# A planned list-and-sort graph kernel: smaller sort pieces with a pause behind each at the end, and a larger hop in the planner

## The chip, the cores and the metric

The kernel runs on one core of one Trainium2 chip. The metric is the device time of one launch in microseconds (us). The engines are called as in the profile: PE is TensorE, DVE is VectorE, ACT is ScalarE, POOL is GpSimd and SP is SyncE. Line numbers (L1332) are lines of the kernel before; the changed file has the same number of lines, so that they hold for both.

## The reference

The input is 16 graphs of 1024 nodes with 64 features each (`x`), a dense 0/1 adjacency matrix for each graph, a node mask (all ones here) and the weights of a small MLP. What is computed, cut to what matters:

```python
h = relu(layernorm(x))
neigh = (adj > 0) & ~eye
rank = exclusive cumsum of neigh along a row;  nb = neighbours of the row
skip = ceil(nb / 2) if nb > 10 else 1
rem = neigh & (skip > 1) & (rank % skip == skip - 1) & mask;  rem |= rem.T
nd = (adj with ones on the diagonal) without rem          # who is left, own node included
s = sort over the nodes left in nd of h, feature by feature
agg = 0.25 * q(s, 0.25) + 0.5 * q(s, 0.5) + 0.25 * q(s, 0.75)   # interpolated quantiles
out = h + agg
y = (relu(out @ W1 + b1) @ W2 + b2) * mask
return x + y
```

So each node gathers the feature rows of the neighbours that are left (some 9 of 1024), sorts them feature by feature, and takes a weighted sum of a few places of the sorted list.

## The kernel before

**Layout.** A batch is one graph. For each of the 16 batches `prepare` (a generator) turns the adjacency matrix into lists of neighbours: `load` (signs L961 on ACT, transposes L968 on PE), `drop` (the removed entries, L1038 to L1049), `keep` (L1061 to L1079), `order` (the nodes ordered by degree, L1085 to L1120) and `collect` (the lists of row numbers `idx`, L1141 to L1210, DVE's MAX8 work). `normalize` (L1255 to L1290) writes relu(layernorm(x)) to a table in DRAM, `gtab`.

**Gathers.** POOL then issues indirect DMAs (L1332 in `fetch`): each takes one column of a list `idx` and brings 128 rows of the table into one slot of a tile. The tiles of a pair of batches (there are 8 pairs) are `g0`, `g1`, `g4` and `g6`, by class of degree; `g0` and `g1` have two buffers, `g4` and `g6` one. The program has 986 gathers and scatters on POOL, and they run one behind the other nearly all the time. A 'place' below counts them from 0.

**Sorts.** `sort` (L1417) takes a tile through a fixed network of steps: minimum and maximum of slots, L1437, L1440 and L1445, on DVE in float32. Then the slots that count are multiplied by coefficients (L1462 on DVE, or L1460 on ACT for the last three pairs, `by_act`), and PE sums them up (L1466). A step over several slots is cut into pieces: most elements per partition in one instruction are `PART` = 384, or `WHOLE` = 1024 with `whole`. Without `whole`, each DVE instruction goes through `opened` (L855): it puts a memset of one column of a small tile `pause` (L859) right behind the instruction; nobody reads `pause`. With `whole` there is no such write. In the kernel before `whole` holds in two places: in `aggregate` (L1547) for the last pair of batches, and in `aggregate_group` (L1707) for the last of two groups. A group is the tile `gg`: the few nodes of a group of 8 batches that have more neighbours than the slots of `g0`.

**The end of the program.** The last pair is sorted in three parts: the tiles g0 and g1 with both batches, then g4 and g6 batch by batch, with the MLP of the first batch (`between` inside `results`) beside the second. Its first slots are not gathered but picked by one-hot matmuls on PE (`pick`, L1376 to L1413, whose DVE part is `hot`, L1392). Memsets (L1525, L1531) and ACT copies (L1528) fill slots ahead of each sort. Behind the last sort come ACT's weights (L1460), PE's sums, the sums by one-hot matrix (`at_p`, L1567 to L1572), two MLP matmuls with their copies, and the output DMA.

**What sets the order.** The program is written as interleaved generators, but the order of each engine's instructions is then set by a planner, `arrange` (L713): it takes all instructions, finds who must be before whom, and walks six times (`ROUNDS`) through the program with a modelled duration for each instruction (`Step.cost`, L605). `forward` (L674) starts at each moment the most urgent instruction that is ready, and `backward` (L695) does this from the end and thereby sets how urgent each is. The order of the best of the six forward walks is kept and tied to each engine. In both walks the time from the end of an instruction to the start of one that depends on it is `between` (L669):

```python
def between(s, o):
    return s.lag + 60 if o.engine != s.engine or s.moves else 115 if s.engine == "DVE" else 0
```

The `lag` is 200 ns for PE, 150 for ACT, 80 for DVE, 950 for a gather and 1500 and more for SP's transfers. So 60 ns stand for a hop between engines or behind a DMA. A pause is no instruction of its own for the planner: it is a tail that makes its instruction 12 ns longer. A 'leash' (`LEASH`) makes a gather wait for a DVE or ACT instruction that was planned to end 25 us before it.

Of the kernel before, what the change touches and what calls it, by code (L numbers as in the profile page):

```python
# [70 lines left out]
GROUP = 8  # L71
SLICE = P // GROUP
SECOND = 14
ROUNDS, LEASH = 6, 25000


TURNED = (0, 1, 3, 2, 0, 1, 3, 2)
# [475 lines left out]
ACTP, ACTB = 5, 13  # L553
# [114 lines left out]

def between(s, o):  # L669

    return s.lag + 60 if o.engine != s.engine or s.moves else 115 if s.engine == "DVE" else 0


def forward(steps, ranks):  # L674
# [138 lines left out]
def list_layer(  # L813
# [15 lines left out]
    B = x.shape[0]  # L829
# [489 lines left out]
    def fetch(m, classes=CLASSES, halves=(0, 1)):  # L1319

        for tiles, slots in classes:
            lo, n = tiles[0], len(tiles)
            held, order = PLANS[slots][:2]

            def begin(h, tiles=tiles, lo=lo, n=n, slots=slots, held=held):
                opening((tiles, slots), m)
                nc.scalar.copy(gathered[m, tiles][:, slots - 1, :, h], owns[m][:, lo:lo + n, h])

            issued, given_out = paced

            def gather(h, slot, k, at, tiles=tiles, lo=lo):
                ins = nc.gpsimd.indirect_dma_start(  # L1332
                    out=gathered[m, tiles][:, slot, k - lo, h], out_offset=None, in_=tables[2 * m + h][0],
                    in_offset=bass.IndirectOffsetOnAxis(ap=lists[2 * m + h][:, at:at + 1], axis=0),
                    element_offset=tables[2 * m + h][1], engine_sem=issued,
                )
                given_out[ins.ins.name] = ins
                return ins

            for h in halves:  # L1340
                queue.append(partial(begin, h))
                for k in tiles:
                    for s, slot in enumerate(order[:FULL[k] + ((k, FULL[k]) in HOSTS)]):
                        if m < pairs - 1 or s >= LEAST[k]:
                            queue.append(partial(gather, h, slot, k, PASSED[k] + s))
# [129 lines left out]
    def terms(acc, out):  # L1475

        for n in range(3):
            to = out[n]
            nc.scalar.copy(to, acc)  # L1479
            if n < 2:  # L1480
                nc.tensor.matmul(acc, minus16, to, start=False, stop=True, skip_group_check=True)
# [14 lines left out]
    def aggregate(m, o, between=None):  # L1496


        last = m == pairs - 1
        coef = coefs[m]  # L1500
        for half in (0, 1) if last else (1, 0):
            parts = CLASSES[2 * half:2 * half + 2][::1 if last else -1]
            for sides in ((0, 1), (1, 2)) if last and half else ((0, 2),):
                hs, one = slice(*sides), sides[0] if last and half else None
                if not one:
                    shape = [P, 4, 2, C] if one is None else [P, 2, 4, C]
                    tag, bufs = ("mx", 3) if last and not half else ("agg", 2)
                    whole = psum.tile(shape, F32, name="acc", tag=tag, bufs=bufs)
                    for tiles, slots in parts:
                        rows, own = slice(tiles[0] - 4 * half, tiles[-1] + 1 - 4 * half), gathered[m, tiles][:, slots - 1]  # L1510
                        nc.tensor.matmul(
                            whole[:, rows] if one is None else whole[:, :, rows], ident32,
                            own if one is None else own.rearrange("p n h c -> p h n c"),
                            start=((tiles, slots) == parts[0]), stop=False, skip_group_check=True,
                        )
                acc = whole if one is None else whole[:, one]
                if one is not None:
                    yield from between(one, False)
                line = {}
                for tiles, slots in parts:  # L1520
                    for k in tiles:
                        for s, slot in enumerate(PLANS[slots][1]):
                            line[k, s] = gathered[m, tiles][:, slot, k - tiles[0], hs]
                            if s >= FULL[k] and (k, s) not in HOSTS:
                                nc.vector.memset(line[k, s], BIG)  # L1525
                for host, guest, first, stop in GUESTS:
                    if host in line:
                        nc.scalar.copy(line[guest][first:stop], line[host][first:stop])  # L1528
                for host, lo, hi in BARE:
                    if host in line:  # L1530
                        nc.vector.memset(line[host][lo:hi], BIG)  # L1531
                for tiles, slots in parts:
                    lo, n = tiles[0], len(tiles)
                    g = gathered[m, tiles]
                    plan = PLANS[slots]
                    if one is None:
                        lines, weigh = g.rearrange("p s n h c -> p s (n h c)"), partial(
                            lambda s, many, lo, n: coef[:, s:s + many, lo:lo + n].rearrange("p s n h -> p s (n h)"),
                            lo=lo, n=n,
                        )  # L1540
                    else:
                        lines, weigh = g[:, :, :, one], partial(
                            lambda s, many, lo, n, h: coef[:, s:s + many, lo:lo + n, h], lo=lo, n=n, h=one
                        )
                    yield from sort(
                        lines, plan, window(tiles, slots)[0], weigh, acc[:, lo - 4 * half:lo - 4 * half + n],
                        m >= ACTP, last,  # L1547
                    )
                    if sides[1] == 2:
                        gathered.pop((m, tiles))  # L1550
                if half and not last:
                    for h in ((0, 1),) if m < pairs - 2 else ((0,), (1,)):
                        fetch(m + 1, CLASSES[2:], halves=h)
                terms(acc, [
                    o[:, 4 * half:4 * half + 4, hs if one is None else one, C * n:C * n + C] for n in range(3)
                ])
                if last and not half:
                    bring_back(m, o)
                if one is not None:
                    yield from between(one, True)  # L1560
# [133 lines left out]
    def aggregate_group(grp):  # L1694
        n = GROUP // 4
        gg = groups.pop(grp)
        to, xg = gathered.pop(("group", grp))
        coef = wk.tile([P, TOP, n], F32, name="gcoef", bufs=1)
        weights(coef, group_num[grp][:, :, 1], n, TOP)
        yield 1.0  # L1700
        tag, bufs = ("mx", 3) if grp == B // GROUP - 1 else ("agg", 2)
        acc = psum.tile([P, n, C], F32, name="gacc", tag=tag, bufs=bufs)
        nc.tensor.matmul(acc, ident32, gg[:, CAP - 1], start=True, stop=False, skip_group_check=True)
        for k in range(n)[::-1]:
            yield from sort(
                gg[:, :, k], PLANS[(CAP, SECOND + 1)[k]], window((0,), CAP)[0],
                lambda s, many: coef[:, s:s + many, k:k + 1], acc[:, k], whole=grp == B // GROUP - 1,  # L1707
            )
        o = wk.tile([P, n * C], F32, name="go", tag="lows", bufs=1)
        nc.scalar.copy(o, acc.rearrange("p k c -> p (k c)"))  # L1710
        yield 0.0
        tp = psum.tile([P, P], F32, name="ot", tag="misc")
        nc.tensor.transpose(tp, o, ident32)
        ot = wk.tile([P, P], F32, name="got", tag="h1", bufs=1)
        nc.scalar.copy(ot, tp)
        yield 0.0
        h1 = wk.tile([P, n, P], F32, name="gh1", tag="highs", bufs=1)
        for k in range(n):
            hp = psum.tile([P, P], F32, name="hp", tag="misc")
            nc.tensor.matmul(hp, w1[k * C:(k + 1) * C], ot[k * C:(k + 1) * C], start=True, stop=True)  # L1720
            nc.scalar.activation(h1[:, k], hp, AF.Relu, bias=b1c)
            yield 0.0
        output(h1.rearrange("p k r -> p (k r)"), n, group_num.pop(grp)[:, :, 0], xg)
        gathered["out", grp], gathered["sum", grp] = (to, xg), o
# [143 lines left out]
def window(tiles, n):  # L1868

    return min(LEAST[k] for k in tiles) // 4, -(-3 * (n - 1) // 4) + 1  # L1870
# [176 lines left out]
```

## Time and profile before

| what | value |
|---|---|
| median of 3 runs | 1443.4 us (1442.67 to 1445.76) |
| time of the profiled execution | 1448.98 us |
| its span in the trace | 1447.2 us |
| mean granted PE clock | 0.898 |
| DVE busy | 1220.1 us (84%) |
| PE busy | 1100.0 us (76%) |
| POOL busy | 1049.3 us (73%) |
| ACT busy | 1041.4 us (72%) |
| first gather on POOL starts, last one ends | 62.77 us, 1412.5 us |

The span runs from the first to the last instruction of the profiled execution. The profiled execution's own time is 1.8 us more than its span, and 5.6 us more than the median. The trace lists each instruction with start and duration; 'idle before' is the time that an engine stood still in front of an instruction, with the name of what ended it. A slice is one fortieth of the span, 36.2 us. Overlapping starts are normal on DVE: an instruction's record begins while the one ahead of it drains, so that the cost of one is read from start to start.

### The profile page before, as it was taken

How to read it: one execution, taken by the hardware profiler on the slowest of the kernel's cores; microseconds unless marked ns; L12 is line 12 of the kernel's file. 1: busy time of each engine (PE TensorE's matmuls, PEld its weight loads, DVE VectorE, ACT ScalarE, POOL GpSimd, SP SyncE). 2: the span in 40 equal slices, each digit the busy share in tenths (PEclk: the TensorE clock that was granted, in tenths of full speed). 3: DMA queues.
4: the chain of work that ended last, by engine and by line, in shares of the span. 5: the costliest groups of instructions: out<-in, count | busy, mean ns of one | idle time of the engine just before them, and what ended most of it. 6: DMA issues, size and time to landing. Idle time of an engine off the chain costs nothing. (4 is left out here: it accounts for less than half of the span.)

```text
span 1447.2 us, 30238 instructions
## 1 busy us (share of the span) xinstructions
PE 1100.0 (76%) x9011; PEld 706.0 (49%) x9011; DVE 1220.1 (84%) x5869; ACT 1041.4 (72%) x2869; POOL 1049.3 (73%) x991
## 2 busy tenths in 40 slices
PE   6877887999888985898479986599837995358167
PEld 4545555555555553555246554365514674125044
DVE  5646799978899899978799898998799779979765
ACT  8797698888959893879558773758839763449554
POOL 0277777777777777777777777777777777778880
PEclk9999998999999997899789997699969998669568
DMA  6453334333524252325332342422211111112110
GB/s 218 141 174 106 111 119 127 90 90 102 148 56 131 64 154 54 100 59 148 91 87 65 88 127 60 118 61 64 69 24 40 32 27 24 24 31 61 35 20 21
DMA packets 128831, 121.67 MB, mean 84 GB/s; under 512 B 95730, under 2 KB 96274, under 8 KB 128658
## 3 DMA queue, kind: packets, MB, share of 16 engines
q1 hardware_dynamic: 97106, 87.29, 19.9%
q0 software_dynamic: 31552, 32.36, 10.2%
q8 instruction: 73, 1.20, 0.3%
q14 instruction: 100, 0.82, 0.2%
HBM read 108.79 MB, written 9.05 MB: 81 GB/s over the span
## 5 line engine op out<-in xcount | busy, mean ns | idle before, releaser
L1332 POOL DMA_INDIRECT g<-gtab,idx x952 | 1013.1, 1064 | 354.3 <-DMA g<-gtab,idx 154.8
L1440 DVE TENSOR_TENSOR g<-g 128x384 f32<-128x384 f32 (+2 forms) x659 | 312.0, 494 | 25.3 <-DMA g<-gtab,idx 19.1
L1445 DVE TENSOR_TENSOR g<-g 128x384 f32<-128x384 f32 (+2 forms) x659 | 310.8, 493 | 5.5 <-DMA gg<-g 4.2
L1145 PE MATMUL codeP<-pack,perm 128*128 128x332 bf16 x1024 | 181.0, 318 | 54.3 <-DVE perm L1120 34.0
L1466 PE MATMUL acc<-g,kf 128*128 128x128 f32 (+2 forms) x472 | 137.6, 424 | 69.0 <-ACT g L1460 46.3
L1048 ACT ACTIVATE dist<-rk,bias 128x512 f16<-128x512 f32 x256 | 169.7, 723 | 23.8 <-DVE bias L1023 10.1
L1145 PEld LDWEIGHTS <-perm 128*128 128x128 bf16 x1024 | 94.1, 100 | 132.8 <-DVE perm L1120 48.2
L981 ACT ACTIVATE ne<-tp 128x512 fp8e4<-128x512 f32 x248 | 144.7, 640 | 12.5 <-PE tp L974 11.1
L1071 ACT ACTIVATE kept<-kp 128x512 fp8e4<-128x512 f32 x224 | 138.4, 642 | 14.3 <-PE kp L1066 5.8
L1460 ACT ACTIVATE g<-g,coef 128x64 f32<-128x64 f32 x336 | 89.2, 359 | 81.4 <-DVE g L1440 63.2
L968 PE MATMUL tp<-kb,sg 128*128 128x128 bf16 x1024 | 107.7, 232 | 47.9 <-ACT dist L1048 27.5
L961 ACT ACTIVATE sg<-at 128x1024 bf16<-128x1024 f32 x122 | 133.8, 1097 | 4.0 <-DMA at<-in_adj_dram 3.9
L1466 PEld LDWEIGHTS acc<-g,kf 128*128 128x128 f32 x472 | 81.5, 210 | 99.2 <-ACT g L1460 56.0
L1038 PE MATMUL rk<-kb,cnt 128*128 128x512 bf16 x256 | 102.2, 399 | 35.9 <-ACT dist L1048 24.1
L1043 PEld LDWEIGHTS <-ne 128*128 128x128 fp8e4 x1024 | 82.2, 101 | 86.0 <-issue 55.9
L859 DVE MEMSET pause<- 128x1 bf16 x2043 | 120.5, 59 | 0.0
L968 PEld LDWEIGHTS <-sg 128*128 128x128 bf16 x1024 | 79.9, 104 | 79.7 <-issue 57.5
L1043 PE MATMUL rk<-kw,ne 128*128 128x128 fp8e5 x1024 | 108.6, 227 | 0.0
L1158 ACT CAST st<-codeP 128x4 bf16<-128x4 f32 x128 | 21.4, 167 | 119.8 <-DVE rest L1156 88.2
L1066 PE MATMUL kp<-kw,rem 128*128 128x128 fp8e5 x1024 | 101.1, 219 | 0.0
L1061 PE MATMUL kp<-ne,kw 128*128 128x512 fp8e4 x256 | 97.5, 382 | 3.5 <-ACT dist L1048 1.4
L1062 PE MATMUL kp<-rem,kw 128*128 128x512 bf16 x256 | 97.5, 381 | 0.0
(202 smaller groups left out, 2371.6 us busy)
## 6 DMA issues: line engine op xcount, KB each, us to landing
at<-in_adj_dram SPq DMA_DIRECT2D x122, 512.0 KB
g<-gtab,idx POOLq DMA_INDIRECT x952
xt<-in_x_dram SPq DMA_DIRECT2D x16, 256.0 KB
y<-in_x_dram SPq DMA_DIRECT2D x16, 256.0 KB
gtab<-xt SPq DMA_DIRECT2D x16, 256.0 KB
out_dram<-y SPq DMA_DIRECT2D x14, 256.0 KB
spare<-in_adj_dram SPq DMA_DIRECT2D x6, 512.0 KB
gg<-g SPq DMA_DIRECT2D x32, 48.0 KB
```

The source lines that it names most:

```text
L859: tails[nc.vector.memset(pause[:, at:at + 1], 0.0).ins.name] = ins.ins.name
L961: nc.scalar.activation(sg, at, AF.Sign)
L968: run.append(nc.tensor.matmul(tp[:, s], sg[:, m * P:(m + 1) * P], ident16, start=(s == 0), stop=(s == 3 and t // 4 != n), skip_group_check ...
L981: nc.scalar.activation(to, tp, AF.Relu, saturate=False)
L1043: run.append(nc.tensor.matmul(rk[:, s * P:(s + 1) * P], ne[:, 4 * n + s, ts], upper, start=False, stop=(s == 3), skip_group_check=True,))
L1048: nc.scalar.activation(dist[:, n * HALF:(n + 1) * HALF], rk, AF.Abs, bias=bias[:, t:t + 1])
L1071: nc.scalar.activation(kept[:, 4 * n:4 * n + 4], kp, AF.Relu, saturate=False)
L1145: run.append(nc.tensor.matmul(flat, perm[:, t, k * P:(k + 1) * P], pack[:, t], start=False, stop=(t == NT - 1), skip_group_check=True,))
L1332: ins = nc.gpsimd.indirect_dma_start(out=gathered[m, tiles][:, slot, k - lo, h], out_offset=None, in_=tables[2 * m + h][0], in_offset=bass ...
L1440: nc.vector.tensor_tensor(at(f + k * df, df, many), pa, pb, OP.min if what == "<" else OP.max)
L1445: nc.vector.tensor_tensor(pa if back else pb, pa, pb, OP.max if what == "<" else OP.min)
L1466: nc.tensor.matmul(acc, ident32, lines[:, s], start=False, stop=(s == now[-1] and not ends), skip_group_check=True)
```

## The change

Three edits. In the planner the 60 ns of a hop become `LATE` = 300 ns, which changes the plan and so may change the order of every engine. The sorts of the last pair and of the last group are no longer `whole`: their pieces hold at most 384 elements per partition, and each of their DVE instructions gets its memset of `pause`.

```diff
-ROUNDS, LEASH = 6, 25000
+ROUNDS, LEASH, LATE = 6, 25000, 300
...
 def between(s, o):
 
-    return s.lag + 60 if o.engine != s.engine or s.moves else 115 if s.engine == "DVE" else 0
+    return s.lag + LATE if o.engine != s.engine or s.moves else 115 if s.engine == "DVE" else 0
...
                     yield from sort(
                         lines, plan, window(tiles, slots)[0], weigh, acc[:, lo - 4 * half:lo - 4 * half + n],
-                        m >= ACTP, last,
+                        m >= ACTP, False,
                     )
...
             yield from sort(
                 gg[:, :, k], PLANS[(CAP, SECOND + 1)[k]], window((0,), CAP)[0],
-                lambda s, many: coef[:, s:s + many, k:k + 1], acc[:, k], whole=grp == B // GROUP - 1,
+                lambda s, many: coef[:, s:s + many, k:k + 1], acc[:, k], whole=False,
             )
```

The two programs, compared instruction by instruction: DVE has 376 instructions more, 344 of them pauses (2387 instead of 2043) and 32 of them because 32 instructions of 128x768 on the last pair's `g1` become 64 of 128x384. The other engines have the same instructions, in another order.

## The prediction

> **What bounds the kernel now.** I read the page first, in part 1 and in the row of POOL in part 2 (tenths of a slice busy, 40 slices).
>
> ```profile
> span 1447.2 us, 30238 instructions
> ...
> PE 1100.0 (76%) x9011; PEld 706.0 (49%) x9011; DVE 1220.1 (84%) x5869; ACT 1041.4 (72%) x2869; POOL 1049.3 (73%) x991
> ...
> POOL 0277777777777777777777777777777777778880
> ...
> L859 DVE MEMSET pause<- 128x1 bf16 x2043 | 120.5, 59 | 0.0
> ```
>
> No engine is full on average, but POOL's row is flat at 7 from the second slice on. In the timeline of POOL the gathers start at 62.77 us and end at 1412.5 us, nearly always 0.30 us after one another; the longest other pause is 1.13 us. An undisturbed gather takes 0.94 us, 1.25 us from start to start. The 64 places from 920 (1301.64 us) to 984 (1412.53 us) take 110.9 us, 1.73 us each; the 920 before them (62.8 to 1301.6 us) took 1.347 us each, and in blocks of 40 between 1.27 and 1.46. So POOL's stream is the bound up to 1412 us, and at its end, where the unpaused sorts run, it is slower. The timeline of POOL there (start, duration, engine, line, in brackets the idle time in front):
>
> ```profile
> 1316.27 0.94 POOL L1332 DMA_INDIRECT g<-gtab,idx  x1 [0.30 <-ACT g L1413]
> 1317.51 3.48 POOL L1332 DMA_INDIRECT g<-gtab,idx  x1 [0.30 <-DVE y L1663]
> 1321.30 1.65 POOL L1332 DMA_INDIRECT g<-gtab,idx  x1 [0.31 <-DMA g<-gtab,idx]
> 1323.25 4.88 POOL L1332 DMA_INDIRECT g<-gtab,idx  x1 [0.30 <-DMA g<-gtab,idx]
> 1328.44 2.24 POOL L1332 DMA_INDIRECT g<-gtab,idx  x1 [0.30 <-DMA g<-gtab,idx]
> 1330.98 1.16 POOL L1332 DMA_INDIRECT g<-gtab,idx  x1 [0.30 <-DVE gg L1445]
> 1332.45 5.14 POOL L1332 DMA_INDIRECT g<-gtab,idx  x1 [0.30 <-DMA g<-gtab,idx]
> ...
> 1372.01 8.20 POOL L1332 DMA_INDIRECT g<-gtab,idx  x1 [0.30 <-DVE gg L1440]
> ```
>
> They wait for nothing; they last longer. Over 0.94 us the 64 gathers have some 30 us in all. Next the table by windows, for the same engines with and without pauses in DVE's stream (columns PE, PEld, DVE, ACT, POOL busy, PE clock, DMA share, GB/s):
>
> ```profile
> 1220.00:1240.00 20.00, 1.09 (x5) 0.35 (x5) 20.00 (x85) 3.08 (x12) 15.73 (x15) 0.50 0.12 24
> ...
> 1317.00:1339.00 22.00, 20.81 (x134) 13.63 (x131) 21.38 (x83) 21.68 (x47) 19.87 (x8) 1.00 0.16 39
> ...
> 1349.00:1381.00 32.00, 7.51 (x34) 7.33 (x34) 31.24 (x64) 9.20 (x16) 27.12 (x17) 0.50 0.07 16
> ```
>
> From 1220 us DVE is full of paused 128x384 operations and 15 gathers fit in 20 us, 1.05 us each. In the other two DVE is as full, unpaused, and 8 gathers fit in 22 us. That is the case for the change. Against it: from 1303 to 1309 us and from 1383 to 1395 us DVE also ran unpaused, and the gathers took 0.94 to 1.05 us. Last the waits of DVE from 1284 us to the end:
>
> ```profile
> DVE g L1440 <- DMA g<-gtab,idx: 12.5, 3, 8.6
> DVE g L1531 <- ACT g L1528: 10.7, 2, 9.0
> ```
>
> The 8.6 us before 1349.45 us and the 9.0 us before 1410.63 us are DVE waiting for late gathers (ACT's copy L1528 of the second waits for one too). After the last gather has landed (1412.9 us) DVE sorts on for 14.5 us, and behind the last sort operation (1428.44 us) ACT, PE, the MLP and the output take 18.8 us to 1447.2 us.
>
> **The pauses and the shorter pieces.** 344 pauses are added; 280 are on operations that stay, 64 on the pieces that 32 operations become. From start to start in the trace an operation of 128 elements takes 0.202 us bare and 0.213 with a pause, one of 256 0.335 and 0.346, one of 384 0.470 and 0.479, one of 768 0.869 (bare only). So a pause costs about 0.0105 us: 280 x 0.0105 = 2.9 us, and 32 x (2 x 0.479 - 0.869) = 2.85 us; together DVE gets 5.8 us more between 1284 and 1428 us.
>
> What they do for POOL the trace shows only by its other stretches. Bounds: at the paused cadences of 1.30 to 1.46 us the 64 places end 16 to 27 us sooner (64 x 1.30 = 83, 64 x 1.46 = 93, against 110.9); if the pauses do nothing, 0. I take the paused cadence, since the 1220 to 1240 us window has the same engine, line and type at full density.
>
> Then DVE is next. From 1284.16 to 1428.44 us it stood idle 23.1 us in the five holes of that stretch and 2.0 in another; its work is 144.3 - 25.1 = 119.2 us. The new order moves a few g0 sort operations from before 1284 us into it (+2.3 us), the pauses add 5.8: 127.3 us, so that the last sort operation ends at 1284.2 + 127.3 = 1411.5 us if DVE never waits. I leave 2.5 us for waits (the holes of 1.64, 1.68 and 2.0 us have other causes than late gathers, and half of them will stay), so 1414.0 us: 14.4 us sooner. For this the last gather must land 14.5 + 0.6 us earlier than that, by 1399 us, which holds at a cadence up to 1.50.
>
> **The new plan.** The value of a hop only matters through the order. Compared by place, DVE's instructions move by 30 on average, ACT's by 4 to 27, PE's by 25, SP's and POOL's hardly. Four places touch a path:
>
> - *Start.* On DVE the mean of batch 1's x (L1262, place 63 before) stands in front of the last `kept` of batch 0 (L1069), and its table work stands ahead of ACT's `dist` operations. In the trace it waits for its load: 3.21 us of DVE idle at 43.58 us. With one or two `kept` operations (0.60 us start to start) now behind that wait, and ACT's table copies (up to 49.49 us before) in front of the path to the first list, the first gather starts some 2.5 us later; bounds 0 and +5 us (SP's load of x is also put ahead of one load of adjacency). As POOL's stream is unbroken from there, this goes through 1:1 to where DVE takes over: +2.5.
> - *Lists 2 and 3.* In front of batch 3's first list DVE now has 22.3 us more work (sorts of pair 0 have moved ahead). It was written at 244.7 us, so now at 267.0. Twelve of its gathers have moved 14 places back on POOL, from 255.0 to what was 274.6 us: 7.6 us are left. Batch 2's list gets 10.6 us more in front of it, and was written at 191.7 us for 228.2: 25.9 us are left. Cost 0, hidden by POOL's other gathers; if the 7.6 us are gone, each further us costs one. Later lists had 50 us and more, buffers 67 us and more.
> - *Scattered.* POOL's rate depends on how full DVE is beside it; the work there is the same. Bounds +-4 us (0.3% of 1238 us, the size by which neighbouring blocks of 40 make up for each other); I take 0.
> - *End.* One ACT copy of the first batch's MLP (L1635) stands behind the last weights L1460: +0.5 us in the end chain. PE, ACT and the output DMA behind the last sort stay, 18.8 us.
>
> Sum against the profiled execution's 1448.98 us: -14.4 + 2.5 + 0.5 = -11.4 us. The median lies 5.6 us below the profiled execution; I carry the difference over: 1443.4 - 11.4 = 1432.0 us.
>
> **A rule that speaks against it.** The Trainium skill ("SBUF — State Buffer", "Who interferes with whom") says that DVE locks GpSimd out of the shared ports for a whole instruction in its two-port modes, and that an operation with two tensor inputs takes only the shared read side and did not hold up descriptor writing where it was probed. By the page the gathers beside min and max of two float32 tensors would not be held up at all, so that a pause could free nothing; the 8.20 us gather between such operations contradicts that, and I go by the row.
>
> **Rivals.**
>
> - *The stalls don't come from missing pauses (slower).* The place is POOL from place 920, the price its cadence. For: the quiet gathers at 1383 to 1395 us; PE and ACT were full from 1317 to 1339 us. Against: PE and ACT were idle mostly from 1349 to 1381 us, with 1.6 us gathers and the one of 8.20 us. Then POOL ends at 1412.5 + 2.5, 14.5 + 0.6 us of DVE follow and the chain has 0.5 more: +3.6 us, 1447.0 us. It decides from a cadence of 1.68 up (each 0.1 us of cadence is 6.4 us).
> - *Half of it.* The stalls get rarer, the cadence stays at 1.58: POOL gains 9.8 us, -9.8 + 3.6 = -6.2 us: 1437 us.
> - *The plan eats the gain.* Batch 3's list comes late by some 9 us and the start by 5: -11.4 + 9 + 2.5 = 0: 1443.5 us. For: the margin is 7.6 us and many small waits add up in front of that list. Against: DVE had holes to take them. With over 12 us late it is slower too.
> - *The edits do nothing but reorder*: the walks are heuristics, and either sign of the scattered 4 us is open; this is inside the others.
>
> **How the numbers follow.** Forecast with its own range (1426 to 1435 us): 0.47. Half of it: 0.24, faster as well. The plan eats the gain: 0.12, of which 0.08 is within 0.2% and 0.02 each on either side. No effect of the pauses: 0.17, of which 0.03 within. A measurement of this kernel can tell about 0.2% (2.9 us) from no change. Faster 0.47 + 0.24 + 0.02 = 0.73; same 0.11; slower 0.02 + 0.14 = 0.16. Low end: no waits of DVE (-2.5), no delay at the start (-2.5), scattered work in favour (-4): 1423 us. High end: no effect of the pauses, 1447 us.
>
> **What would show it.** Right: the gathers after place 920 take 0.94 to 1.15 us with none over 2.5 us, and the stream ends before 1400 us; DVE's holes before L1440 and L1531 shrink to about 2 us; the last sort operation ends near 1416 us, the first gather starts near 65 us and POOL has no hole over 2 us near 270 us. Wrong: gathers of 3 to 8 us beside paused operations; a hole on POOL in front of batch 3's list; a first gather after 68 us; a new hole on DVE behind ACT or PE that holds as long as the gathers did.

## The result and the profile after

The changed kernel takes **1435.07 us** (median of 8 runs, 1432.02 to 1439.88), against 1443.04 us before (8 runs, 1437.3 to 1446.08) in the same measurement: ratio 0.9944, 95% interval 0.9928 to 0.9961, so 8.0 us faster (5.6 to 10.4). The forecast was 1432.0 us, 11.4 us faster, with 1423 to 1447 us as its range. The profiled execution took 1434.8 us, its span is 1433.1 us.

The page of the changed kernel, parts 1 and 2 and the group of the pauses:

```profile
span 1433.1 us, 30572 instructions
...
PE 1128.1 (79%) x9011; PEld 720.0 (50%) x9011; DVE 1223.5 (85%) x6245; ACT 1042.1 (73%) x2869; POOL 1024.4 (71%) x991
...
POOL 0277777777777777777777777777777777777760
...
L859 DVE MEMSET pause<- 128x1 bf16 x2387 | 140.8, 59 | 0.0
```

The same 991 POOL instructions cost 1024.4 instead of 1049.3 us, and POOL's row ends with 760 where it ended with 880: its last gather ends at 1387.6 us, where it ended at 1412.2 us. DVE's busy time grew by 3.4 us only. The table by windows for two stretches of the end (columns as before):

```profile
1317.00:1339.00 22.00, 21.46 (x131) 12.61 (x131) 22.00 (x139) 21.59 (x37) 16.82 (x17) 1.00 0.23 51
1349.00:1381.00 32.00, 14.21 (x60) 11.54 (x58) 31.89 (x173) 25.99 (x58) 25.04 (x22) 0.59 0.19 38
```

In 22 us there are now 17 gathers instead of 8, in 32 us 22 instead of 17, with DVE as full as it was. POOL's timeline has one long gather left:

```profile
1350.96 0.94 POOL L1332 DMA_INDIRECT g<-gtab,idx  x1 [0.30 <-DMA g<-gtab,idx]
1352.77 3.77 POOL L1332 DMA_INDIRECT g<-gtab,idx  x1 [0.87 <-DMA g<-gtab,idx]
1356.84 1.21 POOL L1332 DMA_INDIRECT g<-gtab,idx  x1 [0.30 <-DVE gg L1445]
```

The waits of DVE from 1284 us on, all of them:

```profile
DVE yp L1662 <- PE yp L1658: 8.4, 4, 4.6
DVE highs L1615 <- ACT highs L1614: 0.9, 2, 0.6
DVE highs L1615 <- PE low L1594: 0.9, 1, 0.9
```

The waits for gathers are gone. All that is left, but for 0.3 us, lies behind the last sort operation (it ends at 1411.7 us): from 1284 us to there DVE's holes add up to 0.3 us, where it was 26.8 us before. So DVE has taken over as the bound of the end. The last gather ends 24 us ahead of the last sort operation.

### The profile page after: what moved, and what is told of

It is laid out like the page before. It is cut to its first block, busy times and chain, and to the rows that moved or that the text cites. A ratio compares the mean times of both kernels' runs of the same rounds, so it can differ in the third digit from the quotient of the medians.

```text
span 1433.1 us, 30572 instructions
## 1 busy us (share of the span) xinstructions
PE 1128.1 (79%) x9011; PEld 720.0 (50%) x9011; DVE 1223.5 (85%) x6245; ACT 1042.1 (73%) x2869; POOL 1024.4 (71%) x991
## 3 DMA queue, kind: packets, MB, share of 16 engines
q1 hardware_dynamic: 97106, 87.29, 20.4%
## 4 chain that ended last, share of the span: by engine, by line
issue 30%; ACT 21%; PE 20%; DVE 20%; DMA 5%; POOL 2%; SPq 0%; DVEq 0%; POOLq 0%; ACTq 0%
PE codeP L1145 6%; DVE g L1440 5%; DVE g L1445 4%; ACT dist L1048 4%; DMA g<-gtab,idx 4%; ACT sg L961 3%; ACT ne L981 2%; ACT kept L1071 2%; PE acc L1466 2%; POOL g L1332 2%; PE high L1588 2%; PE low L1594 2%; ACT waste L1238 1%; ACT waste L1243 1%; DVE found L1177 1%
## 5 line engine op out<-in xcount | busy, mean ns | idle before, releaser
L1332 POOL DMA_INDIRECT g<-gtab,idx x952 | 987.2, 1037 | 354.4 <-DMA g<-gtab,idx 163.3
L1440 DVE TENSOR_TENSOR g<-g 128x384 f32<-128x384 f32 (+1 forms) x675 | 312.2, 483 | 25.0 <-DMA g<-gtab,idx 16.2
L1445 DVE TENSOR_TENSOR g<-g 128x384 f32<-128x384 f32 (+2 forms) x675 | 311.7, 482 | 2.3 <-DMA gg<-g 2.2
L1145 PE MATMUL codeP<-pack,perm 128*128 128x332 bf16 x1024 | 189.1, 324 | 9.8 <-DVE perm L1120 7.9
L981 ACT ACTIVATE ne<-tp 128x512 fp8e4<-128x512 f32 x248 | 149.4, 627 | 11.8 <-PE tp L974 7.2
L1071 ACT ACTIVATE kept<-kp 128x512 fp8e4<-128x512 f32 x224 | 134.4, 615 | 15.2 <-PE kp L1066 11.1
L859 DVE MEMSET pause<- 128x1 bf16 x2387 | 140.8, 59 | 0.0
L1066 PEld LDWEIGHTS <-rem 128*128 128x128 bf16 x1024 | 79.3, 99 | 58.4 <-issue 5.4
L1460 ACT ACTIVATE g<-g,coef 128x64 f32<-128x64 f32 x336 | 85.2, 337 | 29.6 <-DVE g L1440 16.3
L1066 PE MATMUL kp<-kw,rem 128*128 128x128 fp8e5 x1024 | 106.6, 222 | 0.0
```

Source lines behind the costliest of these rows:

```text
L981: nc.scalar.activation(to, tp, AF.Relu, saturate=False)
L1066: run.append(nc.tensor.matmul(kp[:, s], rem[:, t, at:at + P], minus, start=False, stop=(s == 3)))
L1071: nc.scalar.activation(kept[:, 4 * n:4 * n + 4], kp, AF.Relu, saturate=False)
L1145: run.append(nc.tensor.matmul(flat, perm[:, t, k * P:(k + 1) * P], pack[:, t], start=False, stop=(t == NT - 1), skip_group_check=True,))
L1332: ins = nc.gpsimd.indirect_dma_start(out=gathered[m, tiles][:, slot, k - lo, h], out_offset=None, in_=tables[2 * m + h][0], in_offset=bass ...
L1440: nc.vector.tensor_tensor(at(f + k * df, df, many), pa, pb, OP.min if what == "<" else OP.max)
```

## The experiments

The theories: **A**, a pause lets a gather go that DVE's unbroken stream holds up, and the end gains by that; **B**, the new order of the instructions makes the gain; and a rival to A, that the smaller piece frees the gathers. Intervals are 95%, against the kernel before on the same chip. 'Rest' is the time from the start of place 920 to the end of the span, 'long' the gathers over 2 us in it (in e1, e9, e2, e10 and e7 one of them is a scatter, an output written from L1752; in e7 it is the longest, and the longest gather took 1.70 us), 'DVE still' its holes over 0.3 us from 1284 us to the last sort operation. These come from one profile each; a profiled execution may lie some us off its median.

| kernel | median, us (runs) | ratio to before | rest | long (longest) | DVE still | last sort to end |
|---|---|---|---|---|---|---|
| before | 1443.04 (8) | 1 | 145.5 | 7 (8.20) | 26.8 | 19.9 |
| e8, before again | 1444.16 (1) | - | 144.6 | 6 (8.21) | 22.0 | 20.0 |
| changed | 1435.07 (8) | 0.9944 (0.9928 to 0.9961) | 134.0 | 1 (3.77) | 0.3 | 21.4 |
| e1, hop alone | 1435.46 (7) | 0.9944 (0.9922 to 0.9966) | 142.8 | 5 (6.34) | 15.5 | 21.5 |
| e9, the same again | 1438.68 (12) | 0.9976 (0.9959 to 0.9994) | 141.2 | 4 (5.86) | 14.4 | 22.2 |
| e2, pieces alone | 1444.10 (12) | 0.9997 (0.9979 to 1.0016) | 144.1 | 2 (17.70) | 14.9 | 21.8 |
| e10, e2 and a pause at the flag | 1441.35 (10) | 0.9987 (0.9969 to 1.0006) | 142.6 | 2 (17.36) | 18.0 | 20.9 |
| e6, e2 with two pauses | 1434.61 (6) | 0.9943 (0.9925 to 0.9961) | 135.0 | 0 (1.31) | 4.1 | 20.4 |
| e3, changed, no pauses | 1455.10 (6) | 1.0081 (1.0054 to 1.0107) | 149.8 | 5 (13.01) | 20.0 | 21.7 |
| e12, changed, two pauses | 1439.24 (12) | 0.9963 (0.9946 to 0.9979) | 137.7 | 0 (1.25) | 1.7 | 21.4 |
| e5, changed, large pieces paused | 1439.92 (12) | 0.9974 (0.9962 to 0.9985) | 135.9 | 1 (8.26) | 7.0 | 23.6 |
| e11, before, every eighth paused | 1432.73 (6) | 0.9928 (0.9904 to 0.9952) | 130.7 | 2 (4.05) | 11.4 | 20.1 |
| e4, before, every one paused | 1429.29 (6) | 0.9900 (0.9875 to 0.9926) | 129.0 | 1 (2.22) | 4.5 | 20.8 |
| e7, before, every third paused | 1427.71 (5) | 0.9895 (0.9877 to 0.9912) | 130.1 | 1 (2.43) | 8.6 | 21.6 |

**The parts by themselves.** e1 undoes both edits of the sorts, e2 the hop:

```diff
e1:  -                        m >= ACTP, False,
     +                        m >= ACTP, last,
     ...                  (and whole=grp == B // GROUP - 1 in aggregate_group)
e2:  -ROUNDS, LEASH, LATE = 6, 25000, 300
     +ROUNDS, LEASH, LATE = 6, 25000, 60
```

> Only the planner's hop is 300; the last pair and the last group are sorted in pieces of up to 1024 elements without pauses, as before. Theory A (the pauses at the end stop DVE from lengthening the gathers, the rest of the change is worth little): long gathers of 3 to 8 us are back behind 1300 us, and the time is that of before within 3 us, 1440 to 1446 us. Theory B (the new order of the instructions brings the gain): as the changed kernel, 1432 to 1438 us.

> Only the sorts of the last pair and the last group are changed (384 elements, a pause behind each); the hop is 60 as before. A: gathers behind place 920 at 1.30 to 1.40 us from start to start, none over 2.5 us, 1432 to 1438 us. B: 1440 to 1446 us.

Both expectations of A missed: the hop alone gives 1435.5 us (1438.7 when it was measured again, e9) and the pieces alone 1444.1. Read as a sum of parts this would say that B is right. The profiles say why it isn't so. In e1 the long gathers are back (4.34, 4.60, 6.34 and 3.19 us, and a scatter of 2.64), as A expects; its order leaves DVE 15.5 us of holes in place of 26.8. In e2 the gathers are short but for one; with it the gain is gone (e6 below has this order without that gather):

```profile
1335.82 1.25 POOL L1332 DMA_INDIRECT g<-gtab,idx  x1 [0.30 <-ACT g L1460]
1337.37 17.70 POOL L1688 DMA_INDIRECT gx<-in_x_dram,gto  x1 [0.30 <-DVE gg L1445]
1355.38 1.21 POOL L1688 DMA_INDIRECT gx<-in_x_dram,gto  x1 [0.30 <-issue]
```

**One thing at a time, in a fixed order.** In e3 and e4 the order of every engine is kept (the planner is given the same durations), and only the pauses of the two sorts are taken away or added:

```diff
e3 (from the changed kernel):
-        gap = (lambda ins: ins) if whole else opened
+        gap = (lambda ins: ins) if whole else unpaused if bare else opened
e4 (from the kernel before):
-        gap = (lambda ins: ins) if whole else opened
+        gap = partial(opened, 0) if whole else partial(opened, 12)
```

`unpaused` only books the 12 ns for the planner, and `bare` marks the two sorts; in e4 `opened` takes the planned cost of its pause first.

> The changed kernel with every engine's order unchanged and pieces of 384, but without the 344 pauses of the last pair's and last group's sorts. A: gathers of 2 to 8 us are back, POOL's stream ends 10 us and more later, 1440 to 1448 us. Rival (it is the smaller piece, not the write behind it, that frees the gathers): no long gathers, and 344 x 0.0105 = 3.6 us less for DVE, 1431 to 1433 us. B: the same as that rival.

> The kernel before with every engine's order unchanged and pieces of up to 1024 elements, but with a pause behind each of the 312 operations of the two sorts. A: the long gathers vanish, last gather before 1400 us, DVE gets 312 x 0.0105 = 3.3 us more and loses the two holes of 8.6 and 9.0 us; 12 us less than before by the profile, 6 to 8 by the medians: 1430 to 1437 us. The rival with the smaller piece and B: no gain, 1443 to 1447 us.

This decides for A where it says that the pauses make the gain. Without the pauses the changed kernel loses 20 us (1455.1 against 1435.07, by medians of different measurements) and is slower than before, more than A expected (1440 to 1448). With them, in the old order and with the large pieces, the kernel before gains 14 us, a little more than A expected (1429.3, against 1430 to 1437). So it is the writes behind the operations that shorten POOL's stream, the smaller piece doesn't: e3 has the small pieces and a gather of 13 us. Here it is, in e3 (8 lines longer: L1340 is L1332, L1539 is L1531), and what DVE did when it ended, at 1379.67 us:

```profile
1366.66 13.01 POOL L1340 DMA_INDIRECT g<-gtab,idx  x1 [0.60 <-DMA g<-gtab,idx]
1379.97 0.94 POOL L1340 DMA_INDIRECT g<-gtab,idx  x1 [0.30 <-DMA g<-gtab,idx]
```

```profile
1377.83 1.01 DVE L1453 TENSOR_TENSOR g<-g 128x384 f32<-128x384 f32 x2
1378.91 0.11 DVE L1539 MEMSET g<- 64x64 f32 x1
1379.05 1.03 DVE L1448 TENSOR_TENSOR g<-g 128x384 f32<-128x384 f32 x2
```

It ends 0.76 us after the start of a memset, the first operation after a run of 68 that read two tensors each, one behind the other; 32 of them began beside the gather. In the profile of before the one of 8.20 us ends at 1380.21 us, 0.75 us after this:

```profile
1379.46 0.11 DVE L1531 MEMSET g<- 64x64 f32 x1
```

Of the 19 other rows over 2 us in e1, e3, e9 and the kernel before, 13 end 0.4 to 0.8 us after the start of such a memset, of a pause of the one-hot operations (L1572), or of an operation that DVE had to wait for (a hole of up to 0.45 us). One ends 0.8 us after DVE ran out of work (2.05 us in e3). The other five have neither a memset nor a hole beside them, and four of these are in the kernel before: its gathers of 3.48 and 2.24 us end 1.03 us after the start of a narrow operation of 128x64, as e3's of 4.65 us does, and those of 4.88 and 5.14 us end 0.90 us after the start of an operation on `yp` (L1662), which lies in PSUM. Here is the narrow one for the 3.48 us gather, which ends at 1320.99 us:

```profile
1319.97 0.21 DVE L1437 TENSOR_TENSOR gg<-gg 128x64 f32<-128x64 f32 x1
```

Nor does an unbroken run hold every gather. In e3 DVE also ran 32 two-input operations on `g` and `gg` in a row from 1341.7 to 1352.8 us, with no memset and no hole, and the 7 POOL transfers that began and ended beside them took 0.97 to 1.17 us each, these two among them:

```profile
1343.61 1.17 POOL L1340 DMA_INDIRECT g<-gtab,idx  x1 [0.30 <-ACT g L1421]
1345.08 1.17 POOL L1340 DMA_INDIRECT g<-gtab,idx  x1 [0.30 <-DMA g<-gtab,idx]
```

So the runs show that the pauses rid the stream of most long gathers; which gather is caught, and what lets it go, they don't settle.

**How many pauses.** e7 and e11 are e4 with a pause behind every third and every eighth operation of the two sorts:

```diff
+    def third(ins):
+
+        seen[0] += 1
+        return ins if seen[0] % 3 else opened(0, ins)
...
-        gap = partial(opened, 0) if whole else partial(opened, 12)
+        gap = third if whole else partial(opened, 12)
```

> The kernel before, order unchanged, pieces of up to 1024, with a pause behind every third operation of the two sorts instead of every one (e4). Theory A (a long gather lasts from one opening in DVE's stream of two-input operations to the next): gathers up to some 2.5 us (three operations of 0.2 to 0.87 us on top of 0.94), cadence behind place 920 of 1.4 to 1.55 us, 1430 to 1437 us. Rival (POOL needs the opening behind each operation, or the openings have to add up): gathers of 3 to 8 us stay, 1438 to 1443 us.

> The kernel before, order unchanged, pieces of up to 1024, with a pause behind every eighth operation of the two sorts. Theory A (a gather is held from one opening to the next): eight operations of 0.2 to 0.87 us are 2 to 5 us, so that gathers of 2 to 5 us are there but the one of 8.2 us is not; between every third (1427.7) and none (1443): 1431 to 1439 us. Rival (any opening now and then is enough): as with every third, under 1430 us.

The rivals' times don't come: a few pauses do most of the work. The longest gather is 8.20 us with no pauses, 4.05 with every eighth, 1.70 with every third and 2.22 with every one; the medians are 1443, 1432.7, 1427.7 and 1429.3 us (e7 a little below A's range). That a gather is held from one opening to the next is not shown as a rule: the 2.22 us gather of e4 outlasted several pauses, and a gather of 2.38 us in e11 ends just ahead of the next one. The 4.05 us gather of e11 (7 lines longer: L866 is L859, L1445 is L1437) ends at 1372.11 us, 0.87 us after the start of the only pause beside it:

```profile
1370.34 0.94 DVE L1453 TENSOR_TENSOR g<-g 128x768 f32<-128x768 f32 x1
1371.22 0.28 DVE L1470 TENSOR_TENSOR gg<-gg,gcoef 128x128 f32<-128x128 f32 x1
1371.24 0.06 DVE L866 MEMSET pause<- 128x1 bf16 x1
1371.42 0.94 DVE L1448 TENSOR_TENSOR g<-g 128x768 f32<-128x768 f32 x1
```

Every third and every one can't be told apart by their times. Both beat the changed kernel.

**Where a pause fails.** In e2 the 17.70 us gather stood beside operations that all had their pause. It began 0.5 us after the flag's operation (L1849) and ended at 1355.08 us, 1.03 us after the start of this narrow operation:

```profile
1336.84 0.15 DVE L1849 TENSOR_SCALAR flag<-fp 1x1 int32<-1x1 f32 x1 [0.30 <-PE fp L1848]
...
1353.85 0.06 DVE L859 MEMSET pause<- 128x1 bf16 x1
1354.05 0.21 DVE L1437 TENSOR_TENSOR gg<-gg 128x64 f32<-128x64 f32 x1
```

e6 puts two pauses behind each operation of the two sorts, e10 one behind the flag's operation:

```diff
e6:  +    def opened_twice(ins):
     ...
     -        gap = (lambda ins: ins) if whole else opened
     +        gap = (lambda ins: ins) if whole else opened_twice if twice else opened
e10: -            nc.vector.tensor_scalar(flag, fp, 0.0, None, OP.is_gt)
     +            free.add(nc.vector.tensor_scalar(flag, fp, 0.0, None, OP.is_gt).ins.name)
     +            at = len(tails) % 64
     +            tails[nc.vector.memset(pause[:, at:at + 1], 0.0).ins.name] = next(iter(free))
```

> The kernel with the pieces alone (hop 60, e2), every engine's order unchanged, with two pauses instead of one behind each operation of the two sorts. In e2 one gather of 17.7 us behind the flag's operation (L1849) stood beside 51 paused operations. Theory A2 (a pause frees a gather only if it falls right, so that a second one helps): no gather over 2.5 us, DVE gets 344 x 0.0105 = 3.6 us more, its hole of 9.9 us goes: 1434 to 1439 us. Rival (that gather reads another table, or the flag's operation holds it): it is again over 10 us long, 1444 to 1448 us.

> The kernel with the pieces alone (e2), order unchanged, with one pause more: behind the flag's operation (L1849), which has none. Theory A2 (the gather of 17.7 us comes from how the pauses fall after the flag's operation, which reads PSUM after a wait): with one more pause the phase is another or the opening is there, the gather is under 4 us and the time 1433 to 1438 us, as with two pauses everywhere (1434.6). Rival (one pause at that place is not enough, since the next 51 did not help): 17.7 us again, 1443 to 1446 us.

With two pauses no gather exceeds 1.31 us, and the time falls to 1434.6 us. With one at the flag the gather is 17.36 us: that expectation fell, though the median of 1441.35 us lies below the rival's range as well, and the profiled run is the slowest of its ten. In the changed kernel, e5, e10 and e2 the long gather is the first to start behind the flag's operation, and each ends 1.03 us after the start of the same 128x64 operation, which comes 2.7, 7.2, 16.3 or 16.7 us after the gather's start. In e3, which has no pauses there, the first gather behind the flag (4.65 us) ends behind that operation too:

```profile
1359.45 0.20 DVE L1445 TENSOR_TENSOR gg<-gg 128x64 f32<-128x64 f32 x1
```

That gather reads `gtab`, as in e5 and the changed kernel, while in e2 and e10 it reads the input, so the table that is read doesn't decide it. Why a single pause fails just there is open; no run separates the flag's operation from the moment in which the stream starts up again behind it.

**Large pieces in the new order.** e5 is the changed kernel with the two `whole` arguments put back and `gap = opened`, so that the large pieces get a pause too.

> The changed kernel (hop 300) with pieces of up to 1024 elements again in the sorts of the last pair and the last group, but a pause behind each. Theory A (the pause does it, the smaller piece only costs DVE 32 x 0.089 = 2.9 us): 2 to 4 us below the changed kernel, 1430 to 1434 us, no gather over 2.5 us behind 1300 us. Rival (which order the planner happens to find decides more than the size of a piece): up to 10 us away on either side, 1425 to 1445 us, with a hole on DVE or a long gather that names the reason.

The rival came true: 8 us above the middle of A's expectation, with one gather of 8.26 us behind the flag's operation. Later ACT waits 6.58 us for a gather, its copies for the group's output (L1715, L1721) come behind that, and DVE stands still for 5.90 us in front of the group's L1662; that the 8.26 us are the cause of this is argued, not tried. From place 920 to the last sort operation e5 takes 112.3 us, as long as the changed kernel (112.6): 6.8 us less work, but 6.5 us more of holes. The 5.1 us by which its span is longer lie elsewhere, 3.2 us ahead of place 920 and 2.2 behind the last sort operation.

**Is DVE the bound now?** e12 is the changed kernel with e6's two pauses, in the changed kernel's order.

> The changed kernel, order unchanged, with two pauses instead of one behind each operation of the two sorts. If DVE is now the bound at the end (its profile shows no hole between 1240 and 1411 us), the longest gather of 3.77 us goes without any gain, and 344 x 0.0105 = 3.6 us more of DVE come through 1:1: 1437 to 1440 us. Rival (POOL's gathers still set the end): no more than before, 1431 to 1436 us.

The 3.77 us gather goes (the longest is 1.25 us) and the kernel gets slower, 1439.24 us: from place 920 to the last sort operation it takes 116.3 us instead of 112.6, though its last gather ends 3.2 us sooner (1384.4 us). That is DVE as the bound. The size is less clean than the expectation: 313 of the 344 new pauses lie in that stretch, DVE's work there grew by 2.5 us (0.008 us for a pause), and the other 1.2 us are new holes, mostly in front of L1662. The 3.77 us gather costs nothing there, since DVE does not wait for it.

**The spread of one kernel.** e8 and e9 are the kernel before and e1 again, unchanged.

> The kernel before, unchanged, for a second profile. If the long gathers depend on the moment at which a gather meets DVE's stream, their places and sum differ from the first profile (31.2 us over 0.94 us each behind place 920) and the time follows them; the rest of the span (first gather, place 920) agrees within 2 us.

> The kernel with the hop of 300 alone (e1) a second time, unchanged: its profiled run (1443.2 us) was the slowest of its seven, the others took 1433.6 to 1438.8. If the hop's order helps by itself, the profile shows from place 920 to the end of the span less than the 142.7 us of the first profile, with fewer long gathers, and the median is again 1434 to 1437 us. If the first profile is typical and the earlier part varies, the same long gathers appear at the same places of the order (4.34, 4.60, 6.34, 3.19, 2.64 us) and the stretch is again some 143 us.

The expectation that the long gathers of before would differ fell: 3.49, 4.88, 2.23, 5.13 and 8.21 us in e8, where they were 3.48, 4.88, 2.24, 5.14 and 8.20; only the last pair differs (2.73 for 2.11 and 3.84). The rest is 144.6 against 145.5 us. Of the 4.8 us between the two spans 3.8 lie ahead of place 920 (1301.6 and 1297.8 us). Of e1's five long rows the second profile has three again (4.60, 3.19 and the scatter of 2.63 us), the first is 5.86 instead of 4.34 us, the one of 6.34 us is missing, and the rest is 141.2 us; the median, 1438.7, is above the 1434 to 1437 us that were expected if the order helps by itself. The hop alone is worth 3 to 8 us by its two medians; where these lie is shown for 2 to 4 of them, in the rest.

## Why the prediction was right, and where its terms were off

- **The gathers and the pauses: right.** Behind place 920 the paused cadence was taken as 1.30 to 1.46 us; it is (1387.9 - 1299.1) / 64 = 1.39 us. e3 and e4 show that the pause does it. "None over 2.5 us" was wrong by the one gather of 3.77 us, and 1.15 us as the upper end by some of 1.2 to 1.3 us.
- **DVE is next: right, and its size as well.** From place 920 to the last sort operation 1414.0 - 1301.6 = 112.4 us were forecast, 112.6 us came, and e12 shows the bound. The 2.5 us left for waits were not needed (0.3 us), so the work itself is some 2 us more than was counted. The price of a pause, 0.0105 us, is right in its size only: in the stretch behind place 920 work grew by 0.008 us for each pause from the changed kernel to e12, and by 0.014 us from the kernel before to e4.
- **The end chain: mis-sized.** I took 18.8 us behind DVE's last operation at 1428.44 us, and +0.5. That operation belongs to the MLP (L1663); the last sort operation ended at 1427.31 us, 19.9 us before the end. After the change it is 21.4 us: the first batch's 16 matmuls `yp` (L1658), done at 1425.7 us before, ahead of the last sums, now run from 1415.3 to 1417.9 us between the last sums and their follow-up on PE. The term should have been +2.6 from 18.8, not +0.5. That these matmuls are the reason is read from the trace, not tried.
- **The start: +2.5 was wrong.** The first gather starts at 62.64 us, against 62.77 and 64.15 in the two profiles of before. The moved operations did not delay it.
- **Lists: right.** No hole on POOL near 270 us; batch 3's gathers start at 271.7 us, 0.30 us after the one in front.
- **Scattered work: 0, as taken**, within what can be told: place 920 starts at 1299.1 us, inside the 1297.8 to 1301.6 of before.
- **From the profile to the median.** By the rest the change gains 134.0 - 145.1 (mean of two) = -11.1 us, where the terms for the end gave -14.4 + 0.5 = -13.9. The two misses (end chain, start) nearly cancel in the forecast of -11.4, which is luck. The medians show -8.0: 1435.07 us lies at the upper edge of the forecast's own 1426 to 1435 us. The remaining 3 us are not explained: they would have to lie ahead of place 920, where two profiles of one kernel differ by 3.8 us.
- **The rivals.** "The stalls don't come from missing pauses" falls by e4. "Half of it" comes near in its time (1437 us) but not in its way: its cadence was 1.58 us. "The plan eats the gain" is not what happened here, but e2 shows it as a danger: there one long gather stands beside a loss of 9.5 us (e2 against e6).
- **The rule that spoke against it.** The prediction weighed half of what the Trainium skill says ("SBUF — State Buffer", "Who interferes with whom"). That two-input operations were not seen to stall DMA is not what these gathers show (e3, e4). But the same section says that an operation with two SBUF inputs contends with a GpSimd instruction that reads SBUF, so the page does not say that such gathers are never held up. A gather takes its row numbers from the SBUF list `idx`; whether that read is what is held, no run here shows.

What the hop brought in the changed kernel, together with the pauses, is an order in which DVE is hardly ever without work from 1284 us to the last sort operation (0.3 us). It is not needed for the gain: e4 and e7 have the old order and are faster.

## What to carry to other kernels

Where a stream of gathers on GpSimd runs beside long runs of two-input VectorE operations, look for gathers that last several times their usual time without waiting; a one-column memset behind every third operation cut the longest from 8.2 to 1.7 us here and gave 1%. Test such an edit with the order of the instructions held fixed: with a planner in between, each part alone gave the opposite picture. And when the stalled stream is freed, the next bound (here VectorE, 112 us of work behind place 920) sets what is gained. The fastest kernels here have large pieces with few or single writes (e7, e4), but in the old order; in the new one large pieces were slower (e5), so that the size of the piece by itself is not settled.

## What the runs showed of the hardware

- A gather of 0.94 us lasted up to 13.0 us beside 32 two-input float32 operations in a row on VectorE, and ended 0.76 us after the start of the first memset (e3). So what holds it lasts longer than one instruction. Yet in the same profile 7 beside 32 other such operations took 0.97 to 1.17 us.
- A long gather can end without a memset or a hole: in the kernel before two end 1.03 us after the start of a 128x64 operation and two 0.90 us after the start of one on a PSUM tile.
- The lengths repeat: 8.20 and 8.21, 4.88 and 4.88 us in two executions of one kernel. They are set by the order of the program more than by chance (of e1's five one was missing the second time and one was longer).
- One write of a single column behind each operation is not always enough (17.7 us in e2, 8.26 in e5); two were, in both kernels tried (1.31 and 1.25 us at most).
